# Layer 1 of a two-layer metaformer: seven of the 25 depthwise taps on GpSimd, sixteen on VectorE, two on TensorE

## The chip, the core and the metric

The kernel runs on one core of a Trainium2 chip. The metric is the device time of one execution in microseconds, lower is better. A core has four engines that compute, each with its own queue that is worked off in order: TensorE (PE; its weight loads are listed as PEld), VectorE (DVE), ScalarE (ACT) and GpSimd (POOL). SP issues transfers. TensorE's products are in PSUM (the kernel uses eight banks of it); the other tiles are in SBUF.

## What is computed

Two images of 96 channels and 96 x 96 pixels go through two layers. Layer 0 (a selective scan behind a deformable sampling, then a quantized FFN) takes most of the time and isn't touched. Layer 1 is this, cut to what matters; its depthwise convolution over the values is `lepe`:

```python
kv = einsum('oc,bchw->bohw', kv_w, x)            # per head: keys, values
k, v = split(kv, 2, axis=2)
x_samp = x.reshape(B, C, hh, 2, ww, 2).mean(axis=(3, 5))
lepe = conv(v, lepe_w, pad=2, feature_group_count=C)   # 5 x 5, one filter a channel
lepe = lepe + lepe_b
attn = softmax(k . q_samp * scale)               # over all 9216 pixels
distribution = v . attn                          # one vector for each of 48 x 48 cells
dmat = softmax(x_unfold . unfold3(x_samp) * dist_scale)   # 9 neighbours
feature = dmat . unfold3(distribution)
out = proj_w . (feature + lepe) + proj_b
```

The layer adds `out` to its input, and then an FFN with two quantized linear layers to the sum.

## The kernel before

For each of the two images, layer 1 has three parts: `_l1_before` (normalization, keys, values and queries), `_l1_attention` (the softmax over all pixels), and the row stage, in which `_l1_rows` is called for eight blocks q of R = 12 rows. The change touches the row stage alone.

A block of the row stage does this. SP loads the normalized rows `xn` (L1677). TensorE makes the values `pv` in four groups (L1697), ScalarE copies them into `vch`, a tile of 16 rows by 100 columns with zero edges that POOL sets (L1684 to L1689). Three times, `near` makes the neighbour softmax on TensorE and ScalarE (`st`, `e`, `pd`, `po`, `rd`), and VectorE multiplies it out into `ft` (L1750). Then come the taps: each tap is a shifted window of `vch` of 12 x 96 = 1152 elements on each of 96 partitions, times one weight for each channel. Taps 0 to 3 (`ON_PE`) aren't computed as taps at all: the output projection is linear, so `_l1_weights` multiplies the projection's weights by the tap's weights (`W.pt`, L1881), and TensorE adds the shifted window of `vch` through them to the projection's sum `pp` (L1781). The other 21 are on VectorE, in `acc`: the first a product (L1762), the other 20 a product and sum in one instruction (L1765), which reads `vch` and `acc` and writes `acc`.

`project` handles each half of 6 rows, in two parts of 288 columns: TensorE sums into one PSUM bank the taps of `ON_PE`, `ft` (L1785) and `acc` (L1791) through the projection; VectorE adds the bias and the layer's input `xr` and so makes `x3` (L1794; the profile calls it x). `_plan_ffn` follows: TensorE and ScalarE normalize, VectorE makes the quantized `fxq` (L900) from PSUM, two linear layers run on TensorE and ScalarE, and at the end POOL adds the FFN's result `fy` to `x` (L940, 96 x 576), and SP stores the rows (L1802).

The order on each engine is written out by a planner (`_Plan`). Each operation is recorded with its engine, a price in us, the tiles it reads and writes, and a due time. The planner simulates the engines with these prices, knows of no other interference between them, and issues in the order of its start times; `_in_order` then holds each engine to that order. Due times make block q's start at 40q. A tile tagged with n buffers holds the planner back until one is free: `vch` has 3, `acc` 2. A tile with `skip` is placed that many elements further in its buffer (L249 to L259). Blocks overlap: while VectorE is at the taps of one block, TensorE and ScalarE are at the FFN of the one before and the values of the next.

Of the kernel before, what the change touches and what calls it, by code (L numbers as in the profile page):

```python
# [14 lines left out]
ALU = mybir.AluOpType  # L15
# [11 lines left out]
C = 96  # L27
HW = 96
# [80 lines left out]
class _Plan:  # L109
# [19 lines left out]
    def op(self, eng, cost, run, r=(), w=(), due=0.0, tab=None, also=(), scan=False, first=False):  # L129
        o = _Op(eng, cost * self.rate.get(eng, 1.0), run, due, tab)  # L130
        o.scan, o.first = scan, first
        ref = lambda t: t if isinstance(t, tuple) else (t, None)
        meets = lambda a, b: a is None or b is None or a == b
        for t, key in map(ref, r):
            o.deps.update(p for p, q in t.writes if meets(key, q))
        for t, key in map(ref, w):
            o.deps.update(p for p, q in t.writes + t.reads if meets(key, q))
        for t, key in map(ref, r):
            t.reads.append((o, key))
        for t, key in map(ref, w):  # L140
            t.writes.append((o, key))
        o.deps.discard(o)
        for t in [x[0] for x in map(ref, list(r) + list(w))] + list(also):
            if t not in o.tiles:
                o.tiles.append(t)
        for t in o.tiles:
            if not t.users and t.tag != "p":
                t.queue.append(t)
            t.users.append(o)
        self.ops.append(o)  # L150
        return o
# [1502 lines left out]


NEAR = 2 * (CELLS + 2)
ON_PE = tuple(range(4))


def _l1_rows(k, P, S, W, ffn, M, distT, x2, out, q, at):  # L1660


    nc = k.nc
    n0 = len(S.ops)
    R = 2 * WIN
# [6 lines left out]
    vch = S.tile(P.wk, [C, R + 4, HW + 4], "vch", 3)  # L1672
# [81 lines left out]
        near(i)  # L1754


    acc = S.tile(P.wk, [C, R, HW], "acc", 2)
    for n, t in enumerate(t for t in range(25) if t not in ON_PE):
        def tap(n=n, t=t):
            src = lambda: vch.ap[:, t // 5 : t // 5 + R, t % 5 : t % 5 + HW]  # L1760
            if n == 0:
                S.op("dve", 0.9, lambda: nc.vector.tensor_scalar(  # L1762
                    acc.ap, src(), W.lw[:, t : t + 1], None, ALU.mult), (vch,), (acc,))
            else:
                S.op("dve", 1.43, lambda: nc.vector.scalar_tensor_tensor(  # L1765
                    acc.ap, src(), W.lw[:, t : t + 1], acc.ap, ALU.mult, ALU.add), (vch,), (acc,))

        tap()

    def project(c2):  # L1770
# [4 lines left out]
        def part(c):  # L1775
# [3 lines left out]
            def some():  # L1779
                for n, t in enumerate(ON_PE):  # L1780
                    nc.tensor.matmul(  # L1781
                        pp.ap[:C, :H2], W.pt[:, n],
                        vch.ap[:, r0 + t // 5 : r0 + t // 5 + 3, t % 5 : t % 5 + HW],
                        start=(n == 0), stop=False)
                nc.tensor.matmul(  # L1785
                    pp.ap[:C, :H2], W.p,
                    ft.ap.rearrange("p i n -> p (i n)")[:, (2 * c2 + c) * H2 : (2 * c2 + c + 1) * H2],
                    start=False, stop=False)

            op("pe", (len(ON_PE) + 1) * H2, some, (vch, ft), (pp,))  # L1790
            op("pe", H2, lambda: nc.tensor.matmul(  # L1791
# [72 lines left out]
def _l1_weights(k, tc, cp, a, W):  # L1864
# [13 lines left out]

    W.pt = cp.tile([C, len(ON_PE), C], F32, tag="pt", name="pt")
    for n, t in enumerate(ON_PE):  # L1880
        nc.vector.tensor_scalar(W.pt[:, n], W.p, W.lw[:, t : t + 1], None, ALU.mult)  # L1881
# [10 lines left out]
def _layer1(k, tc, a, x2d, out):  # L1892
    nc = k.nc
    with ExitStack() as st:
# [18 lines left out]
        for b in range(NB):  # L1913
# [21 lines left out]
            def rows(P, S):  # L1935
                distT = S.tile(P.wk, [128, (CELLS + 2) // 2, C], "distT", 1)
                _l1_turn(k, P, S, M, distT)
                for q in range(CELLS // WIN):
                    _l1_rows(k, P, S, W, ffn, M, distT, x2d[b], out[b], q,
                             lambda v: 40.0 * q + 80.0 * v)  # L1940
# [109 lines left out]
```

## Time and profile before

The three runs took 8306.08, 8321.25 and 8322.18 us; the median is 8321.25.

| | |
|---|---|
| profiled execution, its own time | 8317.46 us |
| its span, first to last instruction | 8315.6 us |
| mean granted TensorE clock | 0.952 |
| PE busy over the span | 7287.6 us, 88% |
| DVE busy | 7623.0 us, 92% |
| ACT busy | 6253.1 us, 75% |
| POOL busy | 5184.1 us, 62% |
| row stage, first image: first to last tap | 6989.7 to 7269.2 us |
| row stage, second image: first to last tap | 7994.4 to 8274.7 us |

In the profile a line such as L1765 is the place in the kernel that issued an instruction. A group of instructions has its count after an x, then busy time and mean nanoseconds of one, then the engine's idle time just before them and who ended it. An instruction's recorded time includes time in which it has started and stands still. TensorE's ends are modelled, so TensorE's busy time isn't a measure of how full it is. The shares over the whole span mix layer 0, in which POOL is busy, with layer 1, in which it mostly isn't; the row stage has to be read by itself.

### The profile page before, as it was taken

How to read it: one execution, taken by the hardware profiler on the slowest of the kernel's cores; microseconds unless marked ns; L12 is line 12 of the kernel's file. 1: busy time of each engine (PE TensorE's matmuls, PEld its weight loads, DVE VectorE, ACT ScalarE, POOL GpSimd, SP SyncE). 2: the span in 40 equal slices, each digit the busy share in tenths (PEclk: the TensorE clock that was granted, in tenths of full speed). 3: DMA queues.
4: the chain of work that ended last, by engine and by line, in shares of the span. 5: the costliest groups of instructions: out<-in, count | busy, mean ns of one | idle time of the engine just before them, and what ended most of it. 6: DMA issues, size and time to landing. Idle time of an engine off the chain costs nothing. (4 is left out here: it accounts for less than half of the span.)

```text
span 8315.6 us, 123907 instructions
## 1 busy us (share of the span) xinstructions
PE 7287.6 (88%) x46090; PEld 3227.2 (39%) x46090; DVE 7623.0 (92%) x5404; ACT 6253.1 (75%) x10610; POOL 5184.1 (62%) x3835
## 2 busy tenths in 40 slices
PE   7888888888888888888888888888878999989998
PEld 3333333333333344333333333333334223542245
DVE  3999999999999999999999999999996998959988
ACT  5777777777777778787777777777746886678867
POOL 4888878788888888888878888888862000110001
PEclk9999999999999999999999999999999999989999
DMA  3554445444444445444444454544441000110001
GB/s 96 164 161 157 151 152 159 145 156 150 154 156 155 150 155 163 153 155 152 157 148 157 145 162 149 159 153 155 152 139 50 3 2 19 33 46 3 2 23 33
DMA packets 359849, 992.21 MB, mean 119 GB/s; under 512 B 69288, under 2 KB 71680, under 8 KB 359040
## 3 DMA queue, kind: packets, MB, share of 16 engines
q1 hardware_dynamic: 357440, 984.04, 37.7%
q8 instruction: 366, 6.00, 0.3%
q14 instruction: 251, 2.06, 0.1%
q10 hardware_dynamic: 1792, 0.12, 0.0%
HBM read 797.19 MB, written 139.25 MB: 113 GB/s over the span
## 5 line engine op out<-in xcount | busy, mean ns | idle before, releaser
L1141 POOL TENSOR_TENSOR h<-h,cre 128x864 f32<-128x864 f32 x2048 | 3486.0, 1714 | 1024.8 <-DVE h L1136 632.0
L1136 DVE TENSOR_TENSOR_SCAN h<-dA,bp 128x864 f32<-128x864 f32 x2048 | 3887.1, 1935 | 157.5 <-PE y L1153 145.9
L1099 ACT ACTIVATE dA<-dlr,A 128x576 f32<-128x576 f32 x3072 | 2156.9, 765 | 1019.6 <-DVE h L1136 914.7
L1119 DVE TENSOR_TENSOR bp<-dur,bp 128x864 f32<-128x864 f32 x2048 | 2062.7, 1045 | 155.3 <-DMA dur<-du_d 46.8
L1153 PE MATMUL y<-h,fold 128*32 128x288 f32 (+2 forms) x18432 | 1776.9, 437 | 103.4 <-POOL h L1141 98.5
L1115 PE MATMUL bp<-bt,selb 128*128 128x288 bf16 x2048 | 619.3, 302 | 690.1 <-DVE h L1136 679.2
L1512 ACT ACTIVATE pr<-sc 128x960 f32<-128x960 f32 (+1 forms) x1080 | 954.1, 937 | 199.7 <-PE sc L1508 178.3
L1153 PEld LDWEIGHTS y<-h,fold 128*32 128x32 f32 x18432 | 726.2, 114 | 746.3 <-POOL h L1141 396.3
L1592 DVE TENSOR_TENSOR sums<-sums,pr 128x3840 f32<-128x3840 f32 (+1 forms) x240 | 959.0, 3996 | 55.6 <-ACT pr L1512 33.1
L1684 POOL MEMSET vch<- 96x32 f32 x16 | 2.5, 154 | 1299.8 <-DVE dist L1546 1207.9
L1115 PEld LDWEIGHTS <-selb 128*128 128x128 bf16 x2048 | 197.4, 96 | 1348.3 <-DVE h L1136 1231.7
L1508 PE MATMUL sc<-qH,kH 32*128 32x480 f32 (+1 forms) x3240 | 627.0, 602 | 9.8 <-DMA q<-qH 5.3
L1197 PE MATMUL y<-selb,minus 128*32 128x288 bf16 x3205 | 598.1, 298 | 0.0
L1508 PE MATMUL sc<-q,kH 32*128 32x480 f32 (+1 forms) x1080 | 564.4, 602 | 0.0
L1574 PE MATMUL av<-pr,vT 128*32 128x480 f32 (+1 forms) x4320 | 533.0, 564 | 3.7 <-ACT av L1599 3.5
L1765 DVE SCALAR_TENSOR_TENSOR acc<-vch,lepe_w,acc 96x1152 f32<-96x1152 f32 x320 | 470.0, 1469 | 8.2 <-ACT vch L1700 0.4
L1508 PEld LDWEIGHTS sc<-qH,kH 32*128 32x128 f32 x3240 | 219.1, 184 | 418.8 <-issue 218.1
L1197 PEld LDWEIGHTS <-minus 128*32 128x32 bf16 x3205 | 272.4, 98 | 263.8 <-issue 192.3
L617 PE MATMUL pc<-xin,w_ca 128*128 128x288 f32 x1152 | 368.5, 423 | 0.1
L940 POOL TENSOR_TENSOR x<-x,fy 96x576 f32<-96x576 f32 x32 | 52.0, 1626 | 477.5 <-ACT fy L939 401.1
L797 PE MATMUL pt<-xd,w_dt 96*128 96x288 f32 x768 | 281.5, 454 | 4.3 <-ACT r L803 1.1
L816 POOL TENSOR_TENSOR e<-e,du 128x576 f32<-128x576 f32 x192 | 231.5, 1206 | 43.7 <-ACT du L812 43.6
(284 smaller groups left out, 10914.1 us busy)
## 6 DMA issues: line engine op xcount, KB each, us to landing
cre<-c_d SPq DMA_DIRECT2D x1024, 288.0 KB, 3.3
dur<-du_d SPq DMA_DIRECT2D x256, 864.0 KB, 5.5
dlr<-dl_d SPq DMA_DIRECT2D x256, 864.0 KB, 5.1
x<-xs SPq DMA_DIRECT2D x512, 72.0 KB, 2.8
du_d<-du SPq DMA_DIRECT2D x128, 288.0 KB, 2.9
dl_d<-dl SPq DMA_DIRECT2D x128, 288.0 KB, 4.0
du_d<-du SPq DMA_DIRECT2D x128, 144.0 KB, 2.5
dl_d<-dl SPq DMA_DIRECT2D x128, 144.0 KB, 3.0
```

Of the source, the lines that this page charges most:

```text
L1099: nc.scalar.activation(dA.ap[:, :, blk, :], dlr.ap[:, blk, :].rearrange("p (c n) -> p c n", c=2), AF.Exp, scale=k.A[:, i, kg, h, blk : blk ...
L1115: nc.tensor.matmul(bp.ap[:, :H2], k.selb[:, kk, i, :], f.bc[o].ap[:, toks], start=True, stop=True)
L1119: nc.vector.tensor_tensor(bp.ap[:, : NBL * H2].rearrange("p (b n) -> p b n", b=NBL)[:, ::-1], dur.ap[:, ::-1, toks], bp.ap[:, :H2].unsquee ...
L1136: nc.vector.tensor_tensor_scan(hv, dv, bv, 0.0, ALU.mult, ALU.add)
L1141: nc.gpsimd.tensor_tensor(ht.ap, ht.ap, cre.ap[:, toks].unsqueeze(1).to_broadcast([128, NBL, H2]), ALU.mult)
L1153: nc.tensor.matmul(dst, k.fold, v, start=False, stop=stop)
L1197: nc.tensor.matmul(P.awake.ap[NBL * CB :, T - HEAD + 2 * 72 : HEAD], k.minus[:, :CB], k.selb[:, 0].rearrange("p i m -> p (i m)")[:, : HEAD ...
L1508: nc.tensor.matmul(two[to // 2][:, to % 2, :n], kH[rows, k0 : k0 + 128], q, start=True, stop=True)
L1512: nc.scalar.activation(pr[:, 2 * i : 2 * i + 2, :n], two[i][:, :, :n], AF.Exp, scale=HD**-0.5)
L1574: nc.tensor.matmul((main if s < HEADS else other)[s * HD : (s + 1) * HD, :n], vT[:, blk, hd, :], pr[:, place(s, p), :n], start=at == 0, st ...
L1592: nc.vector.tensor_tensor(both, both, pr[:, :, :, :n], ALU.add)
L1765: S.op("dve", 1.43, lambda: nc.vector.scalar_tensor_tensor(acc.ap, src(), W.lw[:, t : t + 1], acc.ap, ALU.mult, ALU.add), (vch,), (acc,))
```

## The change

Two of TensorE's four taps and five of VectorE's twenty-one go to POOL, so that POOL has seven, VectorE sixteen and TensorE two (2 and 3). On POOL, product and sum are two instructions: its first tap is a product into `acc`, each of the other six a product into a new tile `one` (two buffers) and a sum of `acc` and `one`. That is thirteen instructions for a block, 7 products and 6 sums, all of 96 x 1152. VectorE's sixteen are all of the form L1765 and come after POOL's in `acc`. `acc` has three buffers in place of two, and lies two elements further in its buffer than `one`. `W.pt` holds two products in place of four, and the sum in `pp` starts with two taps in place of four.

```diff
 NEAR = 2 * (CELLS + 2)
-ON_PE = tuple(range(4))
+ON_PE = (2, 3)
+ON_POOL = (0, 1, 4, 5, 6, 9, 10)
...
-    acc = S.tile(P.wk, [C, R, HW], "acc", 2)
-    for n, t in enumerate(t for t in range(25) if t not in ON_PE):
+    acc = S.tile(P.wk, [C, R, HW], "acc", 3, skip=2)
+    rest = tuple(t for t in range(25) if t not in ON_PE + ON_POOL)
+    for n, t in enumerate(ON_POOL + rest):
         def tap(n=n, t=t):
             src = lambda: vch.ap[:, t // 5 : t // 5 + R, t % 5 : t % 5 + HW]
-            if n == 0:
-                S.op("dve", 0.9, lambda: nc.vector.tensor_scalar(
-                    acc.ap, src(), W.lw[:, t : t + 1], None, ALU.mult), (vch,), (acc,))
-            else:
+            if n >= len(ON_POOL):
                 S.op("dve", 1.43, lambda: nc.vector.scalar_tensor_tensor(
                     acc.ap, src(), W.lw[:, t : t + 1], acc.ap, ALU.mult, ALU.add), (vch,), (acc,))
+                return
+            one = S.tile(P.wk, [C, R, HW], "one", 2, skip=0) if n else acc
+            S.op("pool", 1.5, lambda: nc.gpsimd.tensor_scalar(
+                one.ap, src(), W.lw[:, t : t + 1], None, ALU.mult), (vch,), (one,))
+            if n:
+                S.op("pool", 2.5, lambda: nc.gpsimd.tensor_tensor(
+                    acc.ap, acc.ap, one.ap, ALU.add), (one,), (acc,))
 
         tap()
```

## The prediction, made before the changed kernel ran

> **What bounds the kernel now.** First the page, for what each engine does there; then the windows of the row stage of layer 1, the only stage that the change touches; then its chain; then the timeline of POOL and the groups of POOL, for prices.
>
> ```profile
> span 8315.6 us, 123907 instructions
> ...
> L1765 DVE SCALAR_TENSOR_TENSOR acc<-vch,lepe_w,acc 96x1152 f32<-96x1152 f32 x320 | 470.0, 1469 | 8.2 <-ACT vch L1700 0.4
> ```
>
> The taps take 470 us of VectorE, half of it in each of two row stages (about 6982 to 7307 and 7987 to 8316 us). Windows of the first, in columns of span, PE, PEld, DVE, ACT, POOL, clock, DMA:
>
> ```profile
> 7069.00:7109.00 40.00, 38.18 (x154) 22.69 (x153) 39.42 (x37) 27.61 (x62) 3.22 (x6) 1.00 0.15 43
> 7109.00:7149.00 40.00, 37.70 (x146) 21.91 (x145) 39.49 (x38) 27.27 (x61) 3.12 (x4) 0.96 0.14 38
> 7149.00:7189.00 40.00, 38.64 (x155) 22.53 (x154) 39.47 (x37) 31.05 (x68) 3.77 (x5) 1.00 0.14 41
> ...
> 7270.00:7307.00 37.00, 21.59 (x80) 11.88 (x78) 4.43 (x10) 28.68 (x61) 4.27 (x4) 0.70 0.06 19
> ```
>
> VectorE has under 1 us of 40 free: it is the bound. TensorE is close behind; POOL is nearly idle. The last row is the tail, which starts when the last tap has ended. The chain of waits says the same, and shows more:
>
> ```profile
> 7052.78 1.34 DVE acc L1765
> 7054.14 1.43 DVE acc L1765
> 7055.59 2.33 DVE acc L1765
> 7057.94 1.43 DVE acc L1765
> ```
>
> One tap took 2.33 us where its neighbours took 1.43. POOL at that time:
>
> ```profile
> 7054.92 1.76 POOL L940 TENSOR_TENSOR x<-x,fy 96x576 f32<-96x576 f32 x1 [30.14 <-ACT fy L939]
> ```
>
> POOL's sum started inside the tap of 7054.14 and ended at 7056.68, 1.1 us after that tap; undisturbed it takes 1.27. So it stood still until the tap was done, and then the next tap stood still until POOL was done: the two engines take turns. Other taps of 2.3 us in the chain (7067.45, 7198.15) lie at sums of L940 too. The reader is to see that POOL's idle time here isn't free. Prices for POOL:
>
> ```profile
> L1141 POOL TENSOR_TENSOR h<-h,cre 128x864 f32<-128x864 f32 x2048 | 3486.0, 1714 | 1024.8 <-DVE h L1136 632.0 <-PE y L1153 66.0 <-issue 41.0
> ...
> L816 POOL TENSOR_TENSOR e<-e,du 128x576 f32<-128x576 f32 x192 | 231.5, 1206 | 43.7 <-ACT du L812 43.6
> ...
> L1297 POOL TENSOR_SCALAR xs<-xs 96x144 f32<-96x144 f32 x32 | 18.2, 568 | 2.8
> ```
>
> [...]
>
> **The change, for one block of 12 rows (eight to an image).**
>
> *Sum on POOL.* From 1.206 us at 576 elements and 1.714 at 864 follow 1.764 ns an element; at 1152 that is 1.714 + 0.508 = 2.22 us. Six: 13.3.
>
> *Product on POOL.* Before shows one of 144 elements alone, 0.568 us. [...] From above: 0.568 + 1008 x 1.764 ns = 2.35. I take 1.45[...]. Seven: 10.2. POOL's block is 23.5 us, and 26.0 with two sums of L940; it would fit in a block of now 34.9.
>
> *VectorE's own work.* It loses the product of L1762 (0.81) and four taps of 1.41: 6.45 us. Left are 16 x 1.41 = 22.6, four x (L1794, 0.506), four fxq (0.446) and three ft (0.544) = 5.4: 28.0 us.
>
> *What taking turns costs VectorE.* The sum of 1.27 us lengthened a tap by 2.33 - 1.41 = 0.92, so 0.35 is covered. A long sum then costs 2.22 - 0.35 = 1.87, a product 1.45 - 0.35 = 1.10: 6 x 1.87 + 7 x 1.10 = 18.9 us, and L940 2 x 0.92 = 1.8. Against it, the small instructions (5.4 us) have one input in PSUM and run beside POOL; they hide between none and all of their time. I take 3.5.
>
> *Lead-in.* The first block of an image has no sum to go on with until POOL's part is done: 23.5 us in which VectorE has only ft. Before, its first tap started at 6989.7. Later blocks can have POOL's part done ahead, since acc and vch have three buffers; so seven blocks of eight suffer the turns.
>
> *Tail.* PE, ACT and L940 after the last tap stay: 37 us as before. Some x and fxq fall in it (4.7 us).
>
> *TensorE* loses two of four tap products: 4 groups x 0.98 us = 3.9 of about 33 us a block. VectorE covers that: worth nothing. Two preparations of pt fewer (0.26 us each), also nothing. Memory for one more acc and two "one" costs no time. Transfers (0.15 of the DMA engines) stay; in SP's order out rows go later, and nobody waits for them.
>
> Sum for an image, first to last tap. Before, as a check: 8 x (0.81 + 20 x 1.41 + 5.4) = 275.3, + 160 x 0.055 lengthening = 8.8, - 4.7 in the tail: 279.4; the trace has 6989.7 to 7269.2, 279.5. After: 23.5 + 8 x 28.0 + 8 x 1.8 + 7 x (18.9 - 3.5) - 4.7 = 365. That is +86, for two images +172. The profiled execution took 8317.5 (span 8315.6), and the median of the runs shown is 8321.3, 4 us above it, less than the runs differ. Forecast: 8489 us.
>
> Its own range: [...] with nothing hidden, 390, 8538[...].
>
> **The rivals.**
>
> *Only the two-input sums take turns*, and the products, which read one tensor, do not: 7 x (11.2 - 3.5) = 54, so 311 per image, 8381. For it: no product runs beside a tap in the trace. [...]
>
> *The product is dear* (2.35 us): lead-in 29.8, turns 7 x (11.2 + 14.0 - 3.5) = 152, so 416 per image, 8590. For it: the short product (0.568) is dearer than a sum of the same size at L1295 (0.487). Against: that is one in place on broken rows.
>
> *POOL's queue becomes the bound.* It is in order, and L940 waits there for ACT's fy (197 us in the first image); the next block's products stand behind it, and VectorE waits for them. POOL's block with turns is 26.0 + 15 waits of about 1.2 = 44, next to VectorE's 28.0 + 1.8 + 15.4 = 45.2, so there is no slack. If each of two sums holds the queue for 2 us: 7 x 3.5 = 25 per image, 8538.
>
> *Faster: POOL's time is really free.* The loss at a turn would be a start cost that doesn't grow with the length of POOL's instruction. With no loss beyond today's 8.8: 23.5 + 224 + 8.8 - 4.7 = 252, -28 per image, 8262, if TensorE at some 29 us a block doesn't come first. It decides below 4.0 us lost a block (279.5 - 251.6, over seven), 0.31 for each of 13 instructions. Against: 0.92 was lost at an instruction half as long.
>
> **How the numbers follow.** Turns as worked out 0.55; sums alone 0.12; dear product 0.12; POOL's queue 0.13; free 0.08. The range 8375 to 8590 leaves out the last case and the ends of the others. Under 0.2% (17 us) a measurement can't tell from no change: faster 0.08, same 0.02, slower 0.90.
>
> **What would show it.** Taps of L1765 with a mean near 2.3 us instead of 1.47, and sums on POOL longer than 2.22 by a wait; VectorE still over 90% busy with fewer instructions; blocks of about 45 us; some 23 us of idle VectorE after each attention; TensorE and its tap products shorter with no gain. Taps that stay at 1.47 beside a busy POOL would make it wrong, as would a VectorE that waits long for acc.

## The result, and the profile after

The changed kernel takes 8689.3 us (median of four runs, 8685.1 to 8695.8) against 8321.6 us for the kernel before, measured beside it: a ratio of 1.0451, with a 95% interval of 1.0434 to 1.0467 (the two medians divided give 1.0442, inside it). It is 368 us slower. The forecast was slower too, but by 172 us, and the range ended at 8590.

The page of the changed kernel, its taps and POOL's products among the costliest groups (busy time and mean of one after the bar, then idle time before them):

```profile
span 8683.0 us, 123483 instructions
...
L1764 DVE SCALAR_TENSOR_TENSOR acc<-vch,lepe_w,acc 96x1152 f32<-96x1152 f32 x256 | 714.6, 2791 | 32.7 <-POOL acc L1771 25.9
...
L1768 POOL TENSOR_SCALAR one<-vch,lepe_w 96x1152 f32<-96x1152 f32 x96 | 389.5, 4058 | 0.0
```

L1764 is what L1765 was before. There are 256 taps on VectorE in place of 320, and they take 714.6 us in place of 470: a tap went from a mean of 1.47 to 2.79 us. What stands beside them on POOL is shown by the instructions that touch the tile `one` (count, then minimum, median and maximum duration in nanoseconds):

```profile
L1768 POOL TENSOR_SCALAR one<-vch,lepe_w x96: 3194/4296/4307, 6990.0 to 8612.8; 96x1152 f32<-96x1152 f32 x96
L1771 POOL TENSOR_TENSOR acc<-acc,one x96: 2219/2974/3337, 6993.3 to 8617.2; 96x1152 f32<-96x1152 f32 x96
```

The minimum is what an undisturbed instruction takes: in the first block, up to the first tap at 7022.9 us, all products take 3.19 to 3.21 us and all sums 2.22. The sum is as forecast. The product takes 3.2 us, where the forecast had taken 1.45 and had allowed for 2.35 at most. The median of each is longer by its wait for a tap: 0.75 us on a sum, 1.1 on a product. The other side of these waits stands in the chain of the changed kernel, while the taps of the first block meet POOL's part of the second:

```profile
7031.13 0.03 issue
7031.16 3.27 DVE acc L1764
7034.43 0.03 issue
7034.45 4.01 DVE acc L1764
7038.47 0.03 issue
7038.49 3.27 DVE acc L1764
7041.77 0.03 issue
7041.79 4.01 DVE acc L1764
```

and in POOL's timeline for the same time:

```profile
7030.23 2.97 POOL L1771 TENSOR_TENSOR acc<-acc,one 96x1152 f32<-96x1152 f32 x1
7033.19 4.30 POOL L1768 TENSOR_SCALAR one<-vch,lepe_w 96x1152 f32<-96x1152 f32 x1
7037.57 2.97 POOL L1771 TENSOR_TENSOR acc<-acc,one 96x1152 f32<-96x1152 f32 x1
```

Both engines are at work without a gap by their records, and yet each stands still for the other's instruction in turn: a tap of 1.41 becomes 3.27 beside a sum and 4.01 beside a product. Two taps and one product and sum take 7.34 us together; strictly one after the other they would take 2 x 1.41 + 3.20 + 2.22 = 8.24. Three windows of the row stage (span, PE, PEld, DVE, ACT, POOL, clock, DMA):

```profile
6989.00:7029.00 40.00, 40.00 (x139) 21.77 (x138) 8.76 (x7) 17.74 (x38) 39.50 (x15) 1.00 0.06 15
7029.00:7069.00 40.00, 1.46 (x6) 0.58 (x4) 39.61 (x12) 0.98 (x2) 39.50 (x12) 0.55 0.06 15
...
7149.00:7189.00 40.00, 21.74 (x68) 12.45 (x67) 29.99 (x16) 15.79 (x32) 38.40 (x12) 0.70 0.10 26
```

First comes the lead-in, in which VectorE waits for POOL's first seven taps (8.8 us busy in 40). Then both are full, and TensorE, which waits for the taps, has almost nothing to do: it did 36 to 39 us of work in such a window before. Later, as in the third line, VectorE and POOL each wait in turn for the others: from the end of the lead-in to the last tap, VectorE is busy for 388 of 436 us and POOL for 350.

For the first image, from POOL's first product to the last tap, 6986.8 to 7459.1, it is 472 us, where the kernel before needed 279.5 from tap to tap. In it are a lead-in of 36 us, 357 us of taps, 36 us of VectorE's small instructions after it, and 48 us of other waits of VectorE (the records overlap a little). Of these 48 us, 18 end with the projection's sum (L1797 before L1800), 15 with TensorE's `po` (before L1751) and 5 with POOL's sum.

### The profile page after: what moved, and what is told of

Its sections match the earlier page's. It is cut to its first block, busy times and chain, and to the rows that moved or that the text cites. A ratio compares the mean times of both kernels' runs of the same rounds, so it can differ in the third digit from the quotient of the medians.

```text
span 8683.0 us, 123483 instructions
## 1 busy us (share of the span) xinstructions
PE 7283.4 (84%) x45834; PEld 3211.8 (37%) x45834; DVE 7863.4 (91%) x5322; ACT 6261.3 (72%) x10610; POOL 5898.8 (68%) x4043
## 5 line engine op out<-in xcount | busy, mean ns | idle before, releaser
L1764 DVE SCALAR_TENSOR_TENSOR acc<-vch,lepe_w,acc 96x1152 f32<-96x1152 f32 x256 | 714.6, 2791 | 32.7 <-POOL acc L1771 25.9
L1768 POOL TENSOR_SCALAR one<-vch,lepe_w 96x1152 f32<-96x1152 f32 x96 | 389.5, 4058 | 0.0
L915 ACT CAST fh<-fph 128x288 f16<-128x288 f32 x384 | 141.4, 389 | 195.8 <-PE fph L912 193.7
```

The costliest lines, as they stand in the source:

```text
L1764: S.op("dve", 1.43, lambda: nc.vector.scalar_tensor_tensor(acc.ap, src(), W.lw[:, t : t + 1], acc.ap, ALU.mult, ALU.add), (vch,), (acc,))
```

## The experiments

Three theories stood at the start. TURNS: an instruction on POOL that reads SBUF and a tap on VectorE exclude each other, and the product costs 3.2 us. ORDER: what costs is that POOL's part of `acc` comes first, with the lead-in and the queue waits that follow. WRITES: any work on POOL slows VectorE. Each ratio is to the kernel before, measured on the same chip beside the experiment: 8315.8 us beside the first four, 8322.1 us beside the last four.

**TensorE's part alone.** The kernel before with two taps on TensorE, and so 23 on VectorE.

```diff
-ON_PE = tuple(range(4))
+ON_PE = (2, 3)
```

> TensorE's part of the change alone: its taps go from four to two, nothing goes to POOL, VectorE has 23 taps. Theory TURNS (the two engines take turns at SBUF, and a product on POOL costs 3.2 us): two taps of 1.41 us more in 16 blocks are 45 us on the engine that bounds the stage, 8366 us; mean of L1765 stays at 1.47. Rival ORDER (what costs is the order: POOL's part comes first, and waits in the queues follow): the same, since nothing is on POOL. Rival PE (the change loses because TensorE, with less to do, runs at a lower clock): more than 8400 us, with a clock near 0.7 in the row stage.

Measured: 8341.7 us, ratio 1.0031 (1.0020 to 1.0042), 26 us slower where 45 were expected, with a mean granted clock of 0.947 (so the rival PE is out here); the taps kept a mean of 1.46 us. From the first tap to the last it was 300.5 us in the first image, 21 more than before, as expected; but what follows the last tap, up to the end of the last sum of L940, became shorter, 28 us for 38. Perhaps TensorE, with less to do, trails less behind VectorE at the end of an image; that wasn't tested, and with the planner's other prices (below) the same two taps on TensorE end with 46 us. This part of the change is worth 0.3% of the 4.5%, and TensorE's relief was worth some 19 us of the 45.

**POOL writes and doesn't read.** In the changed kernel, each product becomes a memset of the same length in time (3727 columns of `one`; two shorter ones for a block's first product), and each sum two; issue order, the waits of VectorE for POOL and the number of buffers stay, `one` is longer, and seven taps are left out.

```diff
-            one = S.tile(P.wk, [C, R, HW], "one", 2, skip=0) if n else acc
-            S.op("pool", 1.5, lambda: nc.gpsimd.tensor_scalar(
-                one.ap, src(), W.lw[:, t : t + 1], None, ALU.mult), (vch,), (one,))
+            one = S.tile(P.wk, [C, 3727], "one", 2, skip=0)
+
+            def first():
+                if n:
+                    nc.gpsimd.memset(one.ap, 0.0)
...
+            def second():
+                nc.gpsimd.memset(acc.ap, 0.0)
+                nc.gpsimd.memset(one.ap[:, :1280], 0.0)
+
+            S.op("pool", 1.5, first, (vch,), (one,) if n else (one, acc))
...
```

> POOL's products and sums become memsets of the same length in time (3.2 and 2.2 us), which write SBUF and read nothing; seven taps are left out of the result. Order, dependencies and lead-in stay. TURNS: VectorE's taps go back to a mean of 1.41 to 1.47 us from 2.79, and POOL's own 39 us a block become the bound: 8 x 39 + 23 = 335 us an image from POOL's start to the last tap instead of 472, 8430 us in all. Rival WRITES (any work on POOL slows VectorE): taps stay near 2.8 us, 8690 us. Rival ORDER: taps short or not, the lead-in (36 us) and VectorE's idle time (56 us an image) stay, 8490 us or more.

Measured: 8380.0 us, ratio 1.0070 (1.0054 to 1.0087). VectorE's taps in this kernel, and below them POOL's stand-in for the product:

```profile
L1764 DVE SCALAR_TENSOR_TENSOR acc<-vch,lepe_w,acc 96x1152 f32<-96x1152 f32 x256 | 376.4, 1470 | 102.1 <-POOL acc L1777 95.3
```
```profile
L1771 POOL MEMSET one<- 96x3727 f32 x96 | 307.2, 3200 | 0.0
```

With POOL busy for 39 us of 40 (the mean of the windows from 7069 to 7229), the taps are back at 1.47 us. WRITES falls. VectorE now waits 95 us in two images for POOL, because POOL's block of 39 us is longer than VectorE's own 28; from POOL's start to the last tap it is 328 us (335 were expected). All this, lead-in and waits included, costs 0.70% of the 4.51%; 8430 us were expected, and here too the end of an image is shorter, 30 us for 38. So ORDER can't carry the loss either: what does is what the memsets lack. That is the reading, and with it the arithmetic: no run has POOL read beside the taps without arithmetic, so the runs don't take these two apart.

**Two sums, no dependency.** POOL's taps go into a tile of their own, which TensorE adds through the projection beside `acc`; VectorE starts `acc` with a product.

```diff
-    acc = S.tile(P.wk, [C, R, HW], "acc", 3, skip=2)
+    acc = S.tile(P.wk, [C, R, HW], "acc", 2)
+    accp = S.tile(P.wk, [C, R, HW], "accp", 3, skip=2)
...
+                nc.tensor.matmul(
+                    pp.ap[:C, :H2], W.p, accp.ap[:, r0 : r0 + 3, :], start=False, stop=False)
```

> POOL has a sum of its own (accp), VectorE starts its own (acc) with a product as before the change, and TensorE adds both through the projection: VectorE no longer waits for POOL's part, TensorE has as much to do as with three taps. TURNS: the lead-in goes (36 us an image), taps keep a mean near 2.7 us: 8615 us, between 8580 and 8650. ORDER: lead-in and waits both go, and the time comes back to within 80 us of the kernel before, 8330 to 8400 us.

Measured: 8655.2 us, ratio 1.0408 (1.0390 to 1.0425): 34 us better than the changed kernel, as lead-in and the wait for POOL's part are gone, but not the 290 to 360 that ORDER wanted, and 5 us above the range of TURNS. VectorE's idle time from POOL's first product to the last tap fell from 81 to 20 us an image, but its taps now take 33 us more:

```profile
L1769 DVE SCALAR_TENSOR_TENSOR acc<-vch,lepe_w,acc 96x1152 f32<-96x1152 f32 x240 | 741.0, 3088 | 5.5
L1765 DVE TENSOR_SCALAR acc<-vch,lepe_w 96x1152 f32<-96x1152 f32 x16 | 39.2, 2449 | 17.9 <-ACT vch L1701 9.5 <-DMA xn<-xd 8.1
```

240 taps take longer than the 256 of the changed kernel (714.6 us). From first to last tap it is 439 us in the first image, close to what the turns alone give: six times 7.34 for a product and sum with two taps, 4.02 for the seventh product with a tap, two sums of L940 with a tap at 2.33 each and one tap left over at 1.43 are 54.2 us a block, 433 for eight (an estimate that counts VectorE's small instructions as hidden, and its own product as a tap). The end of an image is longer here, 42 us.

**Real prices for the planner.**

```diff
-                S.op("dve", 1.43, lambda: nc.vector.scalar_tensor_tensor(
+                S.op("dve", 2.79, lambda: nc.vector.scalar_tensor_tensor(
...
-            S.op("pool", 1.5, lambda: nc.gpsimd.tensor_scalar(
+            S.op("pool", 4.06, lambda: nc.gpsimd.tensor_scalar(
...
-                S.op("pool", 2.5, lambda: nc.gpsimd.tensor_tensor(
+                S.op("pool", 2.81, lambda: nc.gpsimd.tensor_tensor(
```

> The changed kernel with the durations of its own trace as the planner's prices: 2.79 for a tap on VectorE, 4.06 and 2.81 for a product and a sum on POOL. Only the order on the engines changes. TURNS: nothing but VectorE's idle time beyond the kernel before can come back, at most 48 us an image: 8590 to 8690 us. ORDER: the planner's wrong prices are the cause, 8500 us or less.

Measured: 8755.9 us, ratio 1.0525 (1.0508 to 1.0543). This is a miss for both theories, since none had the order getting worse: from POOL's first product to the last tap it is 490 us. The taps' mean is a little less (2.60 us), but VectorE waits longer: its idle time in that stretch is 126 us and not 81. Why the planner does worse with these prices was not followed up; that measured durations as prices win the loss back is excluded.

**A quicker product.** The product on POOL as a product of two tensors, the channel's weight repeated along the window.

```diff
-            S.op("pool", 1.5, lambda: nc.gpsimd.tensor_scalar(
-                one.ap, src(), W.lw[:, t : t + 1], None, ALU.mult), (vch,), (one,))
+            S.op("pool", 1.5, lambda: nc.gpsimd.tensor_tensor(
+                one.ap, src(), W.lw[:, t : t + 1].unsqueeze(2).to_broadcast([C, R, HW]),
+                ALU.mult), (vch,), (one,))
```

> The product on POOL is a two-input product with the channel's weight repeated along the window, in place of a product with a per-channel scalar; order and planner's prices as in the changed kernel. TURNS with a dear product: the product falls from 3.2 to about the sum's 2.22 us, each of its turns costs VectorE 0.76 us less (4.02 to 3.26), 49 turns and a shorter lead-in an image: 44 us an image, 8600 us (8570 to 8630). Rival WINDOW (the product is slow because it reads rows of a window): it stays near 3 us, and the time within 30 us of the changed kernel. ORDER: only the lead-in shrinks, 14 us in all, 8675 us.

Measured: 8594.0 us, ratio 1.0334 (1.0318 to 1.0350), 95 us better than the changed kernel for 1.1 us less on each product. The taps' mean fell to 2.50 us, and the longest took 3.27 (the last of the three durations: minimum, median and maximum), so the taps of 4.0 us are gone:

```profile
L1764 DVE SCALAR_TENSOR_TENSOR acc<-vch,lepe_w,acc x256: 1403/3076/3268, 7015.9 to 8553.9; 96x1152 f32<-96x1152 f32 x128
```

It is still 3% slower than the kernel before. WINDOW falls, as this product reads the same windows.

**Prices of POOL's forms.** In the first block of each image, where VectorE is not yet at taps, the products are replaced by other forms; that block's result isn't the convolution.

```diff
+            flat = lambda: xn.ap[:, 2 : 2 + R, :]
+            if q == 0 and n == 1:
+                S.op("pool", 1.5, lambda: nc.gpsimd.tensor_scalar(
+                    one.ap, src(), 0.5, None, ALU.mult), (vch,), (one,))
+            elif q == 0 and n == 2:
...
```

> In the first block of each image, where VectorE isn't at taps, POOL's products are replaced by other forms of the same size, to price them undisturbed; that block's result is no longer the convolution. In the order of the source: immediate scalar from the window; per-channel scalar from a dense tile; immediate scalar from a dense tile; copy of the window; two-input product of window and dense tile; two-input product of window and repeated weight. If the form with a scalar is slow as such, the first three take 3.2 us and the two-input ones 2.2. If the per-channel scalar is what costs, only those with an immediate are quick (under 2 us). If the window costs, only the dense ones are.

POOL's timeline in that block, in the order of the forms:

```profile
6996.23 3.13 POOL L1770 TENSOR_SCALAR one<-vch 96x1152 f32<-96x1152 f32 x1
...
7001.65 3.20 POOL L1773 TENSOR_SCALAR one<-xn,lepe_w 96x1152 f32<-96x1152 f32 x1
...
7007.12 3.12 POOL L1776 TENSOR_SCALAR one<-xn 96x1152 f32<-96x1152 f32 x1
...
7012.50 1.15 POOL L1779 COPY one<-vch 96x1152 f32<-96x1152 f32 x1
...
7015.91 2.62 POOL L1781 TENSOR_TENSOR one<-vch,xn 96x1152 f32<-96x1152 f32 x1
...
7020.79 2.11 POOL L1784 TENSOR_TENSOR one<-vch,lepe_w 96x1152 f32<-96x1152 f32 x1
```

Neither the window nor the per-channel scalar is what costs: a product with a scalar takes 3.1 to 3.2 us in all three forms, dense or not. The two-input product with the repeated weight takes 2.11, and a copy of the same window 1.15. The kernel was executed once (8680.5 us, no interval), and the second image's block has the same durations within 0.01 us.

**Three taps on POOL.** Seven taps become three, (0, 1, 4), and VectorE has twenty.

```diff
-ON_POOL = (0, 1, 4, 5, 6, 9, 10)
+ON_POOL = (0, 1, 4)
```

> Three taps on POOL in place of seven, twenty on VectorE, two on TensorE. TURNS: a block has 3 products and 2 sums and two sums of the FFN to take turns with: 3 x 4.02 + 2 x 3.26 + 2 x 2.33 + 13 x 1.43 = 42 us of taps, and of 5.4 us of small instructions a part: 44 to 46 a block, some 360 us an image against 279.5 before: 8460 to 8510 us. No number of taps pays. ORDER: the lead-in is 14 us and the queue waits are small, 8350 to 8400 us.

Measured: 8492.7 us, ratio 1.0204 (1.0188 to 1.0220). Less the 0.31% of TensorE's part, three taps cost 1.73% and seven 4.20%: 0.58% and 0.60% for each, some 49 us. The turns give the same size: a product and a sum lengthen two taps by 2.61 and 1.85 us, and one tap of 1.41 is saved, 3.05 us in each of 16 blocks, 49 us. That is a rough estimate: the lead-in, the first tap without a sum and what the small instructions hide are left out. So for three and seven taps the loss is in proportion, and the smaller share on POOL only loses less.

**The other engine.** Five taps on TensorE, and POOL as before.

```diff
-ON_PE = tuple(range(4))
+ON_PE = tuple(range(5))
```

> The kernel before with five taps on TensorE and twenty on VectorE, nothing more on POOL: is there anything to gain from the other engine? VectorE gives up 1.41 us a block, TensorE takes 1.95 on top of some 33.5 of 34.9. If VectorE alone bounds the kernel before: 22 us less, 8295 us. If TensorE is as near as its busy time says: within 15 us of the kernel before, either side.

Measured: 8321.2 us, ratio 0.9998 (0.9990 to 1.0007): no difference. VectorE waits more for the projection (L1794 has 39 us of idle time before it in the two row stages; with four taps on TensorE it has 17, with two 6). From the first tap to the last it is 279.7 us, as in the kernel before. The kernel before stands where VectorE and TensorE are about even, and none of the versions run here beats it.

## Why the prediction was right and wrong

*The bound.* VectorE was the bound, and its idle time under 1 us in 40 was read rightly. That TensorE's relief is worth nothing was nearly right: from the first tap to the last hardly anything was gained, but the end of each image became some 10 us shorter, so that the two taps that TensorE gave up cost VectorE 26 us and not 45.

*The turns.* The mechanism was right: the two engines take turns. It was read from one tap of 2.33 us beside one sum of L940 in the kernel before, and the experiment in which POOL only writes confirms it from the other side: the taps fall back to 1.47 us beside a POOL that is just as busy (39 us of 40). The changed kernel's tap of 4.01 us beside a product shows that a product takes turns as well, so the rival in which only two-input sums do so is out. The rival in which POOL's time is free is out by every run in which POOL reads.

*The sum on POOL.* Forecast 2.22 us, measured 2.22; forecast loss at a turn 1.87 us, measured 3.26 - 1.41 = 1.85.

*The product on POOL.* This is the step that failed. The one product in the trace before was of 144 elements, and the step from its 0.568 us to 1.45 us at 1152 elements was the author's estimate, with a slope that no trace or run shows; for its upper bound the forecast took the slope of the sum (1.764 ns). Measured, the slope is (3.196 - 0.568) / 1008 = 2.61 ns, and that decides: on POOL the product with a scalar is dearer per element than the sum. The upper bound, 2.35 us, lay below the 3.20 us measured. The hint was there: at 144 elements the product (0.568) took longer than the sum (0.487), and it was named for the rival "dear product" and then explained away.

*What follows from it.* A product's turn costs 4.02 - 1.41 = 2.61 us and not 1.10, so a block has 6 x 1.85 + 7 x 2.61 = 29.4 us of turns and not 18.9; the lead-in is 36 us and not 23.5. In the forecast's own sum: 36 + 8 x 28.0 + 8 x 1.8 + 7 x (29.4 - 3.5) - 4.7 = 451 us an image in place of 365, +172 and for two images +343, 8661 us. The product's price thus explains 171 of the 196 us by which the measured loss (368) exceeds the forecast one (172). The quicker product moved the time in the expected direction and size (44 us an image expected, 47 measured), so that this step is shown and not only argued. Why the form with a scalar is dear on POOL stays open: the window and the per-channel scalar are excluded.

*What is left.* The other 472 - 451 = 21 us an image are the difference of two errors that partly cancel. VectorE waits 48 us besides the lead-in, which the forecast's sum doesn't have; and its taps are lengthened by 357 - 128 x 1.41 = 177 us, 19 less than the 8 x 1.8 + 7 x (29.4 - 3.5) = 196 of the corrected sum. That 3.5 us a block would be hidden was a guess, and no run isolates it. The engines did keep to one order: in the kernel before, the two row stages (7024 to 7306 us and 8029 to 8312 us) have the same sequence of instructions on TensorE (974), ScalarE (434), VectorE (229) and, but for a memset of `xs` in the first image, POOL (27). The rival of POOL's queue had 25 us an image, and the size is near, but by luck: only 5 of the 48 us end with POOL's sum, 33 with TensorE, which in turn stood idle for 98 us waiting for the taps. Nor is all of the waiting lost: with the dependency gone, VectorE's idle time fell by 61 us an image, of which the taps took back 33 and the longer end of the image 13.

*The tail* was forecast unchanged; from the last tap to the end of the last sum of L940 it went from 38 to 29 us in the first image, as it did with TensorE's part alone (28); why wasn't tested. For two images these 18 us offset much of the 42 us just named, which is how 171 of 196 us can be the product's.

## What to carry to other kernels

An idle engine is only a place for work if its instructions don't exclude those of the engine that is full, as they did here (a tap of 1.41 us became 3.27 or 4.01): look in the trace for an instruction of the full engine that ran beside the idle one, and compare it with its neighbours. Moving a tap to POOL pays here only if its product and its sum lengthen VectorE's other taps by less than the 1.41 us that it saves; the cheapest pair that was run, 2.1 and 2.2 us, lengthened a tap by up to 1.9 us at each of its two turns. And price an operation at its size and in its form: an extrapolation from an eighth of the size needs a slope of its own (the product on POOL took 0.568 us at 144 elements and 3.20 at 1152). Here the small sample contradicted the assumed order of two prices, and the sample was right.

## What the runs showed of the hardware that was not expected

A product with a scalar takes POOL 3.12 to 3.20 us for 96 x 1152 fp32 elements (2.7 to 2.8 ns an element), whether the scalar is a constant or per channel and the source dense or a window; a product of two tensors takes 2.11 (weight repeated) to 2.62 us, and a copy 1.15.

VectorE's own product (TENSOR_SCALAR, 96 x 1152), which takes 0.81 us alone, took a median of 2.59 us in the run with two sums: so it is slowed as well, though it reads one tensor. Instructions of VectorE with one input in PSUM weren't: in the changed kernel's first row stage L1800 has a mean of 0.510 us, L900 (`fxq`) 0.443 and L1751 (`ft`) 0.543, with POOL busy for 348 of 418 us (7022 to 7440), and they had 0.506, 0.445 and 0.544 before.

TensorE's granted clock fell to 0.55 in a window in which TensorE had 1.5 us of work in 40, and the projection's products after it were slower: their median is 687 ns in the changed kernel and 406 ns before. In the changed kernel VectorE waits 18 us for these products in the first image. In the run with two sums the median of this line is 404 ns. What the lower clock costs is not isolated by any run. In the changed kernel VectorE's waits that end with TensorE are 33 us in the first image, out of the 193 us by which its stretch from POOL's first product to the last tap is longer.
